# Turning the rows of an FFN by VectorE and DRAM instead of by TensorE

## Chip, cores and metric

The kernel runs on one core of a Trainium2 chip. The metric is the device time of one execution in microseconds (us); "before" is the median of three runs.

## What is computed

Four sequences of 512 rows with 1024 features each go through causal self-attention with 16 heads, a residual and a normalization, then through one dense layer with int8 weights and a scale per output, a residual and a normalization again. In the reference, cut to what matters here:

```python
x = L0_attn_hidden_states                      # (4, 512, 1024) float32
x = _layernorm(x + _L0_attn_ref(x, w_q, w_k, w_v, w_out), axis=-1)
x = _layernorm(x + _L0_ffn_ref(x, weight, scales), axis=-1)

def _L0_ffn_ref(x, weight, scales):
    w_dequant = weight.astype(jnp.float32) * scales.astype(jnp.float32)[:, None]
    return jnp.einsum('bsi,oi->bso', x, w_dequant)
```

The dense layer is called FFN below. Its matmul needs the rows turned: the features, over which it sums, must lie on the 128 partitions.

## The kernel before, in words

All matmuls run in a one-pass float type (`FR`) on numbers that are split into digits, a high part and a low part, so that together they are as exact as float32. What is multiplied is therefore always a set of tiles "h", "l" and, where both sides are split, a difference "d".

**Attention (from the start to about 765 us).** 32 units (a sequence and a pair of heads) go through projection, scores, softmax and the product with the values. The probabilities and the values are turned by VectorE in 32x32 blocks (`turn`, L445 to L450): the blocks are written to a buffer in DRAM and read back by DMAs that put each block in its place (L457 and L467). The outputs of the heads go to DRAM (`ao`). In this stage the order on TensorE, VectorE and ScalarE is written out by hand.

**Output projection and FFN (from about 740 us on).** The 2048 rows are worked in 16 row tiles t of 128 rows. For each t:

- `load_row` (L188) brings the residual rows into one of four buffers, `x_sb[t]`; the four lie in the former tables `cos_sb` and `sin_sb` and in two staging tiles `row`. A buffer is loaded again once the output of the row tile four back is stored (L651, issued by GpSimd).
- `load_ao` (L184) brings the attention output into `raw_ao`; `high_w` (ScalarE, L212 and L213), `low_w` and `diff_w` (VectorE, L217 and L221) split it into `WD[t % 3]`, which holds h, l and d. There are three such sets.
- `out_product` (L190 to L208) multiplies it with the output weight in two halves of 512 columns, 24 matmuls each (L197, tile `y`). VectorE evacuates each half twice (L206) and adds it to the row; after the last evacuation of half 1, `norm` (L106, L112, L114, L115, L108) normalizes the row.
- `transpose_x1` turns the normed row: eight transposes of 128x128 on TensorE into two PSUM tiles `xT` (L624), then for each half a copy to `x1hi` on ScalarE (L626) and the subtraction `x1lo` on VectorE (L627).
- `ffn` multiplies `x1hi` and `x1lo` with the weight `wf` (L638, 2 x 16 matmuls, tile `f`), scales, adds the residual (L646, L647) and normalizes.

The weight `wf` is cast once from int8 words (L599, L605), half of it on VectorE and half on ScalarE.

In this stage only the order on TensorE is written out by hand (`manual_schedule`, L663): the loop at L664 sets it. In iteration t it lists both projection halves of row tile t + 2, the turn of row tile t and the FFN of row tile t. The first and last iterations differ. In t = 0 the halves (1,1), (2,1) and (3,0) are listed (row tile, half), in t = 1 only (3,1). The halves (0,0), (0,1), (1,0) and (2,0) run earlier, between the attention's last units. In t = 13 the last halves (15,0) and (15,1) are listed, so t = 14 and t = 15 consist of the FFN alone. The order on VectorE, ScalarE and the DMA queue of SyncE (SP) is chosen by a scheduler when the kernel is built. Each engine and each queue works through its list in order, so an instruction that waits holds up all that is behind it.

`x1hi` and `x1lo` come from the pool `row` with one buffer each. For row tile 14 the digits go into `WD[1]`, which is free by then; row tile 15 uses `x1hi` and `x1lo` again. The pool `row` takes the memory of the int8 words, so its tiles can be written only after the casts.

Of the kernel before, what the change touches and what calls it, by code (L numbers as in the profile page):

```python
# [9 lines left out]
FP = mybir.dt.float32  # L10
# [5 lines left out]
ALU = mybir.AluOpType  # L16
AX = mybir.AxisListType

P = 128
B, S, E, H, D = 4, 512, 1024, 16, 64  # L20
NC = E // P
# [17 lines left out]
def attention_ffn_kernel(  # L39
# [18 lines left out]
    nc = tc.nc  # L58
    PSUM = bass.MemoryType.PSUM
# [11 lines left out]
    ident = const.tile([P, P], FP, name="ident")  # L71
# [8 lines left out]
    for n in (512, 384):  # L80
# [5 lines left out]
        out=mask,  # L86
        in_=mask,
# [8 lines left out]
    NT_ROWS = B * NI  # L96
    x_sb, row_tiles, oprod = {}, [], {}
# [3 lines left out]
    def norm(r, name, stats=None):  # L101

        if stats is None:
            stats = stp.tile([P, 2, 6], FP, tag="stats", name=f"stats_{name}")
            for n in range(2):
                nc.vector.bn_stats(stats[:, n, :], r[:, ts(n, 512)])  # L106
        mean, rstd = moments(name, stats)
        nc.vector.tensor_scalar(r, r, mean, rstd, ALU.subtract, ALU.mult)  # L108

    def moments(name, stats):  # L110
        mv = stp.tile([P, 2], FP, tag="mv", name=f"mv_{name}")
        nc.vector.bn_aggr(mv, stats)  # L112
        rstd = stp.tile([P, 1], FP, tag="rstd", name=f"rstd_{name}")
        nc.scalar.activation(rstd, mv[:, 1:2], AF.Sqrt, bias=eps_sb)  # L114
        nc.vector.reciprocal(rstd, rstd)  # L115
        return mv[:, 0:1], rstd
# [10 lines left out]
    R, Q = 4, 32  # L127
# [10 lines left out]
    def digits(name, width):  # L138
        pool = ctx.enter_context(tc.tile_pool(name=name, bufs=1, side=RIGHT_SIDE))
        return [pool.tile([P, NC, width], FR, name=f"{name}_{n}") for n in "hld"]  # L140
# [3 lines left out]
    WD = [digits(f"w{k}", P) for k in (2, 1, 0)][::-1]  # L144
# [36 lines left out]
    def load_ao(t, tile=None):  # L181

        tile = staged["w", t % 3] = stage(f"sa_{t}", [P, NC, P]) if tile is None else tile
        nc.sync.dma_start(out=tile, in_=ao[t // NI][:, :, ts(t % NI, P)])  # L184

    def load_row(t):
        x_sb[t] = row_tiles[t % 4]
        nc.sync.dma_start(out=x_sb[t], in_=x[ts(t, P), :])  # L188

    def out_product(t, half, n, pool, tag):  # L190

        w, r = XD[half], WD[t % 3]
        if n in (0, 2 * NC):
            oprod[n > 0] = pool.tile([P, 512], FP, tag=tag, name=f"y_{t}_{half}_{n}")
        ps = oprod[n >= 2 * NC]
        c, part = (n // 2, n % 2) if n < 2 * NC else (n - 2 * NC, 2)
        nc.tensor.matmul(  # L197
            ps,
            lhsT=r[part][:, c, :],
            rhs=w[part][:, c, :],  # L200
            start=n in (0, 2 * NC),
            stop=n in (2 * NC - 1, NT - 1),
        )
        if n in (2 * NC - 1, NT - 1):
            o = x_sb[t][:, ts(half, 512)]
            nc.vector.scalar_tensor_tensor(o, ps, 1.0 + X12 if n < NT - 1 else -X12, o, op0=MUL, op1=ADD)  # L206
            if half and n == NT - 1:
                norm(x_sb[t], f"a{t}")  # L208

    def high_w(k):  # L210
        t = staged["w", k]
        nc.scalar.activation(WD[k][0], t, AF.Copy, scale=LESS)  # L212
        nc.scalar.activation(t, t, AF.Copy, scale=1.0 / X12)  # L213
# [9 lines left out]
    def split_w(k):  # L223
        low_w(k)
        diff_w(k)
# [380 lines left out]
        nc.gpsimd.tensor_copy(sc32, sc_sb)  # L606

    with tc.tile_pool(name="row", bufs=1) as rowp, tc.tile_pool(name="sum", bufs=2) as sump, tc.tile_pool(
        name="ps_x", bufs=2, space=PSUM
    ) as ps_x, tc.tile_pool(name="ps_f", bufs=2, space=PSUM) as ps_f, tc.tile_pool(  # L610
        name="ps_o", bufs=2, space=PSUM
    ) as ps_o:
        x1T = {}

        def transpose_x1(t, digits=None):


            if digits is None:
                digits = [rowp.tile([P, NC, P], FR, tag=f"x1{n}", name=f"x1{n}_{t}") for n in ("hi", "lo")]
            hi, lo = x1T[t] = digits[:2]  # L620
            for n in range(2):
                ps = ps_x.tile([P, 4, P], FP, tag="xT", name=f"xT_{t}_{n}")
                for c in range(4):
                    nc.tensor.transpose(ps[:, c, :], x_sb[t][:, ts(4 * n + c, P)], ident)  # L624
                cs = slice(4 * n, 4 * n + 4)
                nc.scalar.copy(hi[:, cs, :], ps)  # L626
                nc.vector.tensor_tensor(lo[:, cs, :], ps, hi[:, cs, :], ALU.subtract)  # L627

        def ffn(t, last=False):
            hi, lo = x1T.pop(t)  # L630
            r = x_sb.pop(t)
            stats = stp.tile([P, 2, 6], FP, tag="stats", name=f"stats_f{t}")
            for n in range(2):
                o = ts(n, 512)
                ps = ps_f.tile([P, 512], FP, tag="f", name=f"f_{t}_{n}")
                for c in range(NC):
                    for part in (hi, lo):
                        nc.tensor.matmul(  # L638
                            ps,
                            lhsT=part[:, c, :],  # L640
                            rhs=wfv[:, c, o],
                            start=(c == 0 and part is hi),
                            stop=(c == NC - 1 and part is lo),
                        )
                f = sump.tile([P, 512], FP, tag="sum", name=f"fs_{t}_{n}")
                nc.vector.tensor_mul(f, ps, sc32[:, o])  # L646
                nc.vector.tensor_add(r[:, o], f, r[:, o])  # L647
                nc.vector.bn_stats(stats[:, n, :], r[:, o])
            if not last:
                norm(r, f"f{t}", stats)  # L650
                nc.gpsimd.dma_start(out=out[ts(t, P), :], in_=r)  # L651
                return
            mean, rstd = moments(f"f{t}", stats)
            for n, queue in enumerate((nc.sync, nc.scalar)):
                o = ts(n, 512)
                nc.vector.tensor_scalar(r[:, o], r[:, o], mean, rstd, ALU.subtract, ALU.mult)
                queue.dma_start(out=out[ts(t, P), o], in_=r[:, o])

        def out_half(t, half):
            for n in range(NT):  # L660
                out_product(t, half, n, *((pjp, "pj") if half else (ps_o, "o")))

        with tc.manual_schedule(engines={mybir.EngineType.PE}):  # L663
            for t in range(NT_ROWS):  # L664
                early = t + 2
                if 1 < t < NT_ROWS - 2:
                    out_half(early, 0)
                if t + 3 < NT_ROWS:
                    if t:
                        load_row(t + 3)  # L670
                    load_ao(t + 3, raw_ao)
                    high_w(t % 3)
                    split_w(t % 3)
                if t == 0:
                    out_half(1, 1)
                    transpose_x1(0)
                    out_half(2, 1)
                    out_half(3, 0)
                elif early < NT_ROWS:
                    transpose_x1(t)  # L680
                    out_half(early, 1)
                if t == NT_ROWS - 3:

                    transpose_x1(t + 1, WD[t % 3])
                if t == NT_ROWS - 2:
                    transpose_x1(t + 1)
                ffn(t, t == NT_ROWS - 1)


# [44 lines left out]
```

## Time and profile before

| What | Value |
|---|---|
| median of three runs | 1058.34 us (1056.18 to 1058.88) |
| the profiled execution's own time | 1059.0 us |
| its span, first to last instruction | 1057.2 us |
| TensorE (PE) busy | 1013.2 us, 96% |
| VectorE (DVE) busy | 891.1 us, 84% |
| ScalarE (ACT) busy | 384.2 us, 36% |
| GpSimd (POOL) busy | 185.4 us, 18% |
| mean granted TensorE clock | 0.992 |
| share of the chain of waits: the transposes xT, L624 | 1% |
| xT: matmuls, mean length | 128 (in three groups), 272 to 273 ns |
| x1hi copies on ScalarE (L626) | 32, 588 ns |
| x1lo subtractions on VectorE (L627) | 32, 677 ns |

"Busy" is the time in which an engine works on an instruction; matmuls are pipelined, so their lengths overlap and their sum is more than the time they take up. The chain of waits is followed back from the last instruction: at each step it goes to what released it, or to the instruction before it on the same engine. It says which work sets the end. The granted clock is TensorE's clock as a share of full speed.

### The profile page before, as it was taken

To read this page: it belongs to the slowest core of one execution; us is meant where nothing else is said; L and a number is where in the kernel's file an instruction comes from. 1 tells how busy PE (TensorE), PEld (TensorE's weight loads), DVE (VectorE), ACT (ScalarE), POOL (GpSimd) and SP (SyncE) were. 2 spreads that over 40 slices of the span, in tenths; PEclk is the share of its full clock that TensorE was granted. 3 is DMA by queue.
4 is the path that set the end of the run, shared out by engine and by line. 5 is a ranking of instruction groups with operands and counts; after the bars stand their busy time and mean duration, and the time that the engine had idled before them with its cause. 6 is when DMAs were issued, how large, how long until landed. Compare 5 with 4: busy or idle time off the path is not lost.

```text
span 1057.2 us, 13527 instructions
## 1 busy us (share of the span) xinstructions
PE 1013.2 (96%) x4708; PEld 754.4 (71%) x4708; DVE 891.1 (84%) x1386; ACT 384.2 (36%) x854; POOL 185.4 (18%) x281
## 2 busy tenths in 40 slices
PE   9989999999999989999999999988799999999997
PEld 3666777767777667677776777765588888888885
DVE  6998898998989989898898988988897767667666
ACT  5524354343544334444344443443342121121110
POOL 0122232222322222232223322221200000000000
PEclk9999999999999999999999999999999999999999
DMA  6556655766557766566655666577532222221201
GB/s 258 162 186 191 189 179 179 225 194 179 179 181 223 240 203 191 158 209 190 211 187 159 210 195 210 183 214 245 178 120 104 77 100 80 80 80 60 77 23 60
DMA packets 192212, 173.65 MB, mean 164 GB/s; under 512 B 90640, under 2 KB 156688, under 8 KB 192016
## 3 DMA queue, kind: packets, MB, share of 16 engines
q1 hardware_dynamic: 184656, 155.22, 47.0%
q10 hardware_dynamic: 5328, 9.70, 2.5%
q0 software_dynamic: 2160, 7.87, 1.8%
q8 instruction: 37, 0.61, 0.2%
q14 instruction: 31, 0.25, 0.1%
HBM read 105.64 MB, written 67.11 MB: 163 GB/s over the span
## 4 chain that ended last, share of the span: by engine, by line
PE 67%; DVE 21%; ACT 4%; DMA 3%; issue 2%; POOL 0%; SPq 0%; DVEq 0%; ACTq 0%
PE p L267 31%; PE y L197 15%; PE f L638 11%; PE o L475 6%; DVE nmx L415 4%; DVE s L412 3%; DVE w_l L217 3%; DVE w_d L221 2%; PE s L398 2%; DVE pr L448 2%; PE xT L624 1%; ACT sw L213 1%; DVE x_d L175 1%; ACT w_h L212 1%; DVE rot L235 1%
## 5 line engine op out<-in xcount | busy, mean ns | idle before, releaser
L267 PE MATMUL p<-x_h,w_h 128*128 128x512 f32 x736 | 290.5, 395 | 0.0
L267 PE MATMUL p<-x_l,w_l 128*128 128x512 f32 x736 | 287.0, 390 | 0.5 <-DVE w_l L217 0.5
L443 POOL TENSOR_SCALAR pr<-pr,rden 128x128 f32<-128x128 f32 (+3 forms) x256 | 175.0, 703 | 572.1 <-DVE rden L437 533.4
L267 PE MATMUL p<-x_d,w_d 128*128 128x512 f32 x736 | 186.1, 395 | 0.9 <-DVE v L309 0.9
L429 ACT ACTIVATE pr<-s,nmx 128x128 f32<-128x128 f32 (+3 forms) x256 | 132.4, 539 | 147.8 <-DVE nmx L415 111.9
L267 PEld LDWEIGHTS p<-x_h,w_h 128*128 128x128 f32 x736 | 138.1, 188 | 52.5 <-issue 22.7
L267 PEld LDWEIGHTS p<-x_d,w_d 128*128 128x128 f32 x736 | 135.7, 188 | 33.9 <-issue 5.1
L267 PEld LDWEIGHTS p<-x_l,w_l 128*128 128x128 f32 x736 | 138.3, 188 | 28.9 <-DVE w_l L217 0.9
L286 ACT ACTIVATE tA<-p 128x512 f32<-128x512 f32 x92 | 55.8, 606 | 219.2 <-PE p L267 219.2
L197 PE MATMUL y<-x_h,w_h 128*128 128x512 f32 x256 | 102.7, 401 | 4.4 <-DVE row L206 3.9
L415 DVE TENSOR_REDUCE nmx<-s 128x2 f32<-128x256 f32 (+3 forms) x128 | 102.5, 821 | 3.4
L475 PE MATMUL o<-prT,va 128*64 128x256 f32 (+3 forms) x512 | 79.4, 454 | 24.6 <-ACT pr L429 21.2
L197 PE MATMUL y<-x_l,w_l 128*128 128x512 f32 x256 | 101.2, 395 | 1.0 <-DVE w_l L217 1.0
L448 DVE STREAM_TRANSPOSE pr<-pr 128x768 f32<-128x768 f32 (+1 forms) x96 | 100.0, 1049 | 0.9 <-POOL pr L443 0.8
L638 PE MATMUL f<-wf,x1hi 128*128 128x512 f32 x240 | 93.6, 390 | 0.0
L638 PE MATMUL f<-wf,x1lo 128*128 128x512 f32 x240 | 93.6, 390 | 0.0
L475 PEld LDWEIGHTS o<-prT,va 128*64 128x64 f32 x512 | 34.9, 140 | 73.8 <-issue 37.1
L309 DVE SCALAR_TENSOR_TENSOR raw<-p,tA 128x512 f32<-128x512 f32 x61 | 40.2, 659 | 50.8 <-PE p L267 50.8
L398 PE MATMUL s<-qk 64*128 64x384 f32 (+3 forms) x512 | 79.4, 450 | 1.8 <-DVE qk L242 1.8
L221 DVE TENSOR_TENSOR w_d<-w_h,w_l 128x1024 fp32r<-128x1024 f32 x60 | 73.7, 1228 | 1.5
L197 PE MATMUL y<-x_d,w_d 128*128 128x512 f32 x256 | 64.2, 392 | 1.4 <-DVE v L309 0.7
L197 PEld LDWEIGHTS y<-x_h,w_h 128*128 128x128 f32 x256 | 48.7, 190 | 16.0 <-DVE row L206 4.3
(105 smaller groups left out, 1225.2 us busy)
## 6 DMA issues: line engine op xcount, KB each, us to landing
turned<-pr SPq DMA_DIRECT2D x64, 384.0 KB, 2.3
turned<-pr SPq DMA_DIRECT2D x32, 512.0 KB, 3.7
prT<-turned SPq DMA_DIRECT2D x32, 512.0 KB, 4.9
prT<-turned SPq DMA_DIRECT2D x32, 384.0 KB, 4.7
turned_v<-v SPq DMA_DIRECT2D x32, 256.0 KB, 3.3
va<-turned_v SPq DMA_DIRECT2D x128, 64.0 KB, 2.6
prT<-turned SPq DMA_DIRECT2D x32, 256.0 KB, 3.6
ao<-ot ACTq DMA_DIRECT2D x32, 256.0 KB, 2.0
```

The costliest lines, as they stand in the source:

```text
L197: nc.tensor.matmul(ps, lhsT=r[part][:, c, :], rhs=w[part][:, c, :], start=n in (0, 2 * NC), stop=n in (2 * NC - 1, NT - 1),)
L221: nc.vector.tensor_tensor(d, h, l, SUB)
L267: nc.tensor.matmul(ps, lhsT=w[part][:, c, :], rhs=r[part][:, c, :], start=n in (0, 2 * NC), stop=n in (2 * NC - 1, NT - 1),)
L286: nc.scalar.activation(prod["tA"], ps, AF.Copy, scale=1.0 + X12)
L309: nc.vector.scalar_tensor_tensor(raw_tile(u, k), ps, -X12, prod["tA"], op0=MUL, op1=ADD)
L398: nc.tensor.matmul(ps[:, j, at : at + n], lhsT=t[rows, 0, ts(i, P)], rhs=keys[rows, :, : (i + 1) * Q], start=True, stop=True,)
L415: nc.vector.tensor_reduce(nmx[:, 2 * i : 2 * i + 2], ps[:, :, at : at + n], AX.X, ALU.max, negate=True)
L429: nc.scalar.activation(pr[:, :, at // P : at // P + i + 1, j, :], ps[:, j, at : at + n].rearrange("p (r k s) -> p r k s", r=R, s=Q), AF.Ex ...
L443: nc.gpsimd.tensor_scalar(p, p, rden[:, m : m + 1], 1.0, ALU.mult, ALU.mult)
L448: nc.vector.transpose(t, t)
L475: nc.tensor.matmul(ps[j * D : (j + 1) * D, kb * P :], lhsT=v[:, kb, 2 * j : 2 * j + 2, :].rearrange("p a s -> p (a s)"), rhs=t[:, :, 4 * k ...
L638: nc.tensor.matmul(ps, lhsT=part[:, c, :], rhs=wfv[:, c, o], start=(c == 0 and part is hi), stop=(c == NC - 1 and part is lo),)
```

## The change

The normed rows are turned in the way of `turn` in the attention. VectorE turns the row in 32x32 blocks into a new tile `blocks` (one buffer); one DMA of SP writes it to one of two buffers in DRAM, `turned_x`, and four DMAs read it back, each 128 KB in pieces of 32 numbers, straight into `x1lo`. ScalarE then copies the whole tile to `x1hi`, and VectorE subtracts it in place. TensorE takes no part. The two PSUM tiles of the transposes are gone.

Read back in this way the features lie on the partitions in another order: partition p holds the feature p % 4 * 32 + p // 4 of each block of 128. The rows of the int8 weight are put into the same order when the inputs are prepared. The digits of row tile 15 go into `WD[2]` instead of `x1hi` and `x1lo`, and its turn is listed one iteration earlier, beside that of row tile 14.

```diff
         def transpose_x1(t, digits=None):
             if digits is None:
                 digits = [rowp.tile([P, NC, P], FR, tag=f"x1{n}", name=f"x1{n}_{t}") for n in ("hi", "lo")]
             hi, lo = x1T[t] = digits[:2]
-            for n in range(2):
-                ps = ps_x.tile([P, 4, P], FP, tag="xT", name=f"xT_{t}_{n}")
-                for c in range(4):
-                    nc.tensor.transpose(ps[:, c, :], x_sb[t][:, ts(4 * n + c, P)], ident)
-                cs = slice(4 * n, 4 * n + 4)
-                nc.scalar.copy(hi[:, cs, :], ps)
-                nc.vector.tensor_tensor(lo[:, cs, :], ps, hi[:, cs, :], ALU.subtract)
+            blocks = rowp.tile([P, R, NC, Q], FP, tag="blocks", name=f"blocks_{t}")
+            nc.vector.transpose(blocks, x_sb[t].rearrange("p (c r s) -> p r c s", r=R, s=Q))
+            nc.sync.dma_start(
+                out=turned_x[t % 2].rearrange("a (n r) w -> (a n) (r w)", r=R),
+                in_=blocks.rearrange("p r c s -> p (r c s)"),
+            )
+            x1 = lo.bitcast(FP)
+            for a in range(R):
+                nc.sync.dma_start(
+                    out=x1[:, :, ts(a, Q)], in_=turned_x[t % 2][a].rearrange("p (c s) -> p c s", s=Q)
+                )
+            nc.scalar.copy(hi, x1)
+            nc.vector.tensor_tensor(lo, x1, hi, ALU.subtract)
...
                 if t == NT_ROWS - 3:
                     transpose_x1(t + 1, WD[t % 3])
-                if t == NT_ROWS - 2:
-                    transpose_x1(t + 1)
+                    transpose_x1(t + 2, WD[(t + 1) % 3])
                 ffn(t, t == NT_ROWS - 1)
...
-        "w8": rows(L0_ffn_weight).reshape(P, NC * E).view(np.int32),
+        "w8": np.ascontiguousarray(rows(L0_ffn_weight)[np.arange(P) % 4 * 32 + np.arange(P) // 4]).reshape(P, NC * E).view(np.int32),
```

`R` is 4, `Q` is 32, `NC` is 8, `P` is 128 and `NT_ROWS` is 16.

## The prediction, made before the changed kernel ran

> **What bounds the kernel now.** I read the busy table and the chain of waits first, then the chain and the timelines of the stage that the diff touches, from 755 us to the end. The chain of that stage, in order of time (start us, length us, what):
>
> ```profile
> 770.99 0.87 PE xT L624 x8
> 771.87 10.93 PE y L197 x48
> 782.80 7.38 PE f L638 x32
> 790.18 0.87 PE xT L624 x8
> 791.05 5.49 PE y L197 x24
> 796.54 7.26 PE f L638 x32
> 803.80 5.49 PE y L197 x24
> 809.29 0.87 PE xT L624 x8
> ```
>
> TensorE alone carries the chain until 1049.7 us, without a wait between its pieces. One row of steady state is a projection half y (24 matmuls, 5.49), the turn xT (0.87), the other half (5.49) and the FFN f (7.26). VectorE has room, as the busy time by stretch shows (stretch, then PE, PEld, DVE, ACT, POOL busy):
>
> ```profile
> 850.00:870.00 20.00, 20.00 (x93) 16.58 (x92) 13.62 (x23) 3.79 (x6) 0.53 (x1) 1.00 0.27 91
> ```
>
> So a turn taken off TensorE is worth its full chain time, as long as its replacement is ready when TensorE reaches f.
>
> **What is removed.** 128 transposes (16 rows of 8), 32 ScalarE copies (0.59 each) and 32 VectorE subtractions (0.68). Their matmul row by kind reads
>
> ```profile
> L624 PE MATMUL xT<-ident,row 128*128 128x128 f32 x64 | 8.3, 273 | 0.0
> ```
>
> 273 ns each. The Trainium skill ("TensorE: Matmul & The Clock Gate", Part 4: PE-mode transpose) gives a transpose about 275 ns within a kernel. By that length the change would save 128 x 0.273 = 34.9 us. The chain decides otherwise: eight of them take 0.87, since they overlap, so the saving is 16 x 0.87 = **13.9 us**. I take 13.9.
>
> **What is added, per row.** On VectorE one 32x32 turn of 128x1024 (L448 does the same size in 1.24) and one subtraction of 128x1024 (L171: 1.21). On ScalarE one copy of 128x1024 (L212: 1.06). On SP one write of 512 KB to DRAM (row loads of that size land 3.2 after issue, row stores 2.9; I take 3.0; ends 2.3, the 384 KB row of L449, and 3.7, its 512 KB row) and four reads of 128 KB in pieces of 128 bytes. The nearest row to the reads is L467, with pieces of the same size, half as many:
>
> ```profile
> va<-turned_v SPq DMA_DIRECT2D x128, 64.0 KB, 2.6
> raw_ao<-ao SPq DMA_DIRECT2D x13, 512.0 KB, 4.1
> 738.41 2.55 SPq L467 DMA_DIRECT2D va<-turned_v x4
> ```
>
> The last line is SP's timeline (start, length of four issues: 0.64 each). So four va reads are through at 3 x 0.64 + 2.6 = 4.5 us; the DMA share over that time adds up to about 2.0 us of work on all 16 engines. The new reads have twice the pieces, about 4.0 us of work, behind about 1.7 us of latency: **5.7 us** for a set (ends 4.5, as if the pieces cost nothing, and 8, as if issue and work added up). VectorE sees in all 16 x (1.24 + 1.21) - 32 x 0.68 = +17.4 us over some 290 us, which fits into its free third. ScalarE's load hardly moves (16 x 1.06 for 32 x 0.59).
>
> **Where the wait falls.** x1lo and x1hi have one buffer, and the reads land in x1lo. So the reads of row t wait until the FFN of row t-1 has read its last x1lo. From there to the FFN of row t there lie two projection halves, 10.98 us, in rows 2 to 13, but only one, 5.49, in row 1. Before the change the matmul into PSUM needed no such release.
>
> *Rows 2 to 13.* Reads 5.7, copy 1.06, subtraction 1.21, with 0.3 of handovers: 8.3 of 10.98. VectorE's list has the subtraction after the evacuations of projection half 0 (L206, done at about 7.2 by its queue) and ahead of those of half 1 (the first is available at about 9.1), so it is neither late nor in the way. On SP, ahead of the reads stand a row load (it waits for a store that ended some 9 us after the FFN before) and an ao load (issued about 4 us before); both are out of the way. The write of the turned blocks is issued a whole row early. Cost 0, with 2.7 us to spare.
>
> *Row 0.* Here nothing has to be released, but the order does the harm. The timeline of VectorE before:
>
> ```profile
> 776.72 3.34 DVE L605 CAST wf<-words 128x1024 fp32r<-128x1024 int8 x4
> 779.99 0.68 DVE L206 SCALAR_TENSOR_TENSOR row<-y,row 128x512 f32<-128x512 f32 x1
> 780.70 0.69 DVE L106 BATCH_NORM_STATS2 stats_a<-row 128x6 f32<-128x512 f32 x1
> ```
>
> In the changed program's instruction list the turn of row 0 stands behind these three, although row 0 was normed at 769.3: it begins at 781.4 and ends at 782.65. The write lands at 785.75. SP then has the ao load of row 6 ahead of the four reads; it waits for low_w of row 5, which VectorE's list places after the turn and two evacuations: 785.35. So the reads are issued from about 785.95, behind 512 KB whose work is about 2.6 us: 785.4 + 1.7 + 2.6 + 4.0 = 793.7 if they queue wholly, 791.65 if not; I take 793.0. Copy and subtraction: 795.4. TensorE, rid of one turn, is at f at 782.63 - 0.87 = 781.76. **Stall 13.6 us** (ends: write 2.3 and reads 4.1 give 10.7; write 3.7 and full queueing give 15.6).
>
> *Row 1.* From the end of FFN 0: reads 5.8. VectorE takes the rest of FFN 0's norm, two evacuations (L206), low_w and only then the subtraction of row 1. In the trace before, the evacuation of FFN 0's second half starts at 790.21 and low_w ends at 798.4; in that measure, projection half (3,1) ends at 796.4, and the subtraction would end at 799.7. **Stall 3.4** (3.3 to 5).
>
> *Row 15.* The last projection half leaves two FFNs, 14.5 us. Row 14's subtraction is now queued ahead of the last evacuation and holds it about 1.2 us; evacuation and norm 2.9 (1025.94 to 1028.8 without the subtractions); turn 1.24, write 3.0, reads 5.7, copy and subtraction 2.3: 16.4. **Stall 1.9** (0 to 4).
>
> **The clock.** A stall costs more than itself. In TensorE's timeline (start, length, instruction, idle before):
>
> ```profile
> 377.70 4.07 PE L475 MATMUL o<-prT,va 128*64 128x512 f32 x16 [3.43 <-DMA va<-turned_v]
> 755.68 0.50 PE L197 MATMUL y<-x_h,w_h 128*128 128x512 f32 x1 [3.88 <-DVE row L206]
> 756.72 0.57 PE L197 MATMUL y<-x_h,w_h 128*128 128x512 f32 x1
> 760.08 0.44 PE L197 MATMUL y<-x_h,w_h 128*128 128x512 f32 x1
> ```
>
> From 756.72 to 760.08 eight matmuls started 0.42 apart instead of 0.227, at a granted clock of 0.50: 1.6 us lost after 3.88 idle. After 3.43 idle (377.7) the clock was 0.50 again. The skill's rule against the change is in "TensorE: Matmul & The Clock Gate", Why this matters for your kernels: no idle gaps of more than about 3 us. By the rule both stalls, 13.6 and 3.4, are charged: +3.2. By the rows alone the second lies just below the shortest gap of its kind, and the charge could be 1.6. The nearest row is 3.43, so I charge both. Gaps of 1.67 and 2.11 left the clock alone, one of 1.83 (at 56.5) didn't; for row 15 I charge nothing (end 1.6).
>
> **Sum.** -13.9 + 13.6 + 3.4 + 1.9 + 3.2 = **+8.2 us**. On the profiled execution (1059.0, of which the span is 1057.2) that is 1067.2; it lay 0.7 above the median of the runs, so for the median 1058.34 + 8.2 = 1066.5. Low ends: -13.9 + 10.7 + 3.3 + 0 + 1.6 = +1.7, 1060.0. High ends: -13.9 + 15.6 + 5 + 4 + 6.4 (two slow windows after row 0, one after each other stall) = +17, 1075.4.
>
> **Rivals.** A difference below 0.3% (3.2 us) can't be told from none.
>
> 1. *Slower by the stalls of rows 0, 1 and 15*, +8.2: chance 0.70.
> 2. *The cover nearly holds: no change or better.* One mechanism: the round trip of row 0 through DRAM. If the ao load ahead doesn't delay the reads and a set takes 4.5, the first stall is about 11, and with no clock charge for row 1 and row 15 on time the sum is about +2, near 1060.5; it decides from 17 us of stalls and clock charges in all downward, and the change is faster by over 3.2 only from 10.7 downward, which the stall of row 0 alone uses up. For it: the DMA engines are idle three quarters of this stage. Against it: the turn of row 0 waits behind the casts whatever the DMAs do. Chance 0.17, of which 0.06 for faster (about 1050).
> 3. *Every row stalls.* If a set of reads takes over 8.4 us, each of rows 2 to 13 waits, and VectorE's queue is held by the subtraction: at 9.5 about 12 x 1.1 = 13 us more, and two to three more in rows 0 and 15: 1082. For it: pieces of 128 bytes, and SP's issues are in one queue with the ao and row loads. Against it: the va reads. Chance 0.13.
>
> The range takes case 1 with its ends and most of case 2: 1060 to 1075. Slower 0.81, same 0.13, faster 0.06.
>
> **What would show it.** In the profile after: a TensorE gap of 10 to 16 us ahead of the first f, ended by the subtraction into x1lo, then a granted clock of 0.5; a second gap of 3 to 5 ahead of the second f; none in rows 2 to 13, with rows 18.2 apart instead of 19.1; one of about 2 before the last f. A first gap below 6 us, or gaps in the rows between, would prove me wrong, and so would rows that are still 19.1 apart.

## The result, and the profile after

| What | Before | After |
|---|---|---|
| median of four runs | 1058.26 us (1056.18 to 1058.88) | 1067.24 us (1065.45 to 1069.31) |
| ratio of the times | | 1.0086, 95% interval 1.0061 to 1.0111 |
| span of the profiled execution | 1057.2 us | 1067.5 us |
| TensorE busy | 1013.2 us | 1005.4 us |
| VectorE busy | 891.1 us | 908.9 us |
| mean granted TensorE clock | 0.992 | 0.980 |

The change makes the kernel 9.0 us slower by the medians and 10.3 us slower by the two profiled spans. TensorE has less to do and yet ends later, so it waits. The chain of waits of the changed kernel, in the stage that the diff touches (start us, length us, what), shows where:

```profile
777.98 3.33 DVE wf L605 x4
...
782.55 0.15 DVE blocks L624
...
786.48 0.53 SPq L184
...
787.10 0.62 SPq L631
...
790.47 3.64 DMA x1lo<-turned_x
794.21 1.05 ACT x1hi L634
795.29 1.24 DVE x1lo L635
796.57 8.49 PE f L646 x31
...
811.19 1.22 DVE w_l L217
812.40 1.14 DVE x1lo L635
813.59 10.14 PE f L646 x31
823.73 10.92 PE y L197 x48
...
841.92 10.92 PE y L197 x48
```

Before, this stretch was TensorE alone. Now the chain leaves TensorE twice, ahead of the FFN of row 0 and ahead of the FFN of row 1. From row 2 on it is TensorE alone again, and there the rows are 841.92 - 823.73 = 18.19 us apart where they were 19.11. That is 0.92 gained per row, 14.7 in sixteen rows. The two FFNs behind the gaps are also longer: 31 matmuls of 32 (the first one ran within the gap) would take 31/32 of 7.26, which is 7.03, and took 8.49 and 10.14. Not all of that is a slow clock: in five of the kernels below 31 matmuls behind a wait took 7.29 to 7.34 although the granted clock stayed at 1.00.

TensorE's timeline has the same waits with what ended each (start, length, instruction, and in brackets the idle time before it and its releaser):

```profile
795.31 0.79 PE L646 MATMUL f<-wf,x1hi 128*128 128x512 f32 x1 [12.12 <-ACT x1hi L634]
796.57 0.79 PE L646 MATMUL f<-wf,x1lo 128*128 128x512 f32 x1 [0.47 <-DVE x1lo L635]
811.75 0.49 PE L646 MATMUL f<-wf,x1hi 128*128 128x512 f32 x1 [1.21 <-ACT x1hi L634]
813.59 0.79 PE L646 MATMUL f<-wf,x1lo 128*128 128x512 f32 x1 [1.35 <-DVE x1lo L635]
...
1042.66 0.47 PE L646 MATMUL f<-wf,w_h 128*128 128x512 f32 x1 [0.69 <-DVE fs L654]
1051.23 0.49 PE L646 MATMUL f<-wf,w_h 128*128 128x512 f32 x1 [0.86 <-ACT w_h L634]
1052.49 0.50 PE L646 MATMUL f<-wf,w_l 128*128 128x512 f32 x1 [0.77 <-DVE w_l L635]
```

I measure a gap from the end of the work before it to the second matmul of f, the one with x1lo, and take off 0.23 for the first matmul, which runs within it.

- Row 0: from 795.31 - 12.12 = 783.19 to 796.57 is 13.4, net 13.15.
- Row 1: from 810.54 to 813.59 is 3.05, net 2.8.
- Row 15: from 1050.37 to 1052.49 is 2.1, net 1.9.
- Row 14: 0.69 ahead of its f, ended by VectorE's late evacuation of the FFN before it.

Rows 2 to 13 have no wait at all. The granted clock is in the busy time by stretch of the changed kernel (stretch, then length, PE, PEld, DVE, ACT and POOL busy, granted clock, DMA share, GB/s):

```profile
795.30:799.10 3.80, 3.33 (x7) 2.33 (x8) 2.37 (x2) 0.00 (x0) 0.00 (x0) 0.50 0.17 66
813.00:819.40 6.40, 5.81 (x14) 4.55 (x15) 4.60 (x7) 0.29 (x1) 0.00 (x0) 0.50 0.62 199
...
850.00:870.00 20.00, 20.00 (x90) 16.52 (x89) 15.61 (x24) 4.74 (x6) 0.53 (x1) 1.00 0.53 145
```

These stretches lie inside longer spells: the clock is at half from 785.49 to 799.14, of which only the last 2.6 us lie behind the second matmul of row 0's f, and from 812.80 to 819.62, of which 6.0 us do so in row 1. In row 15's FFN it is 1.00 throughout. The last line answers to the one shown of before: in a steady 20 us VectorE is busy 15.6 us instead of 13.6, still with room.

The sum by this trace: -14.7 for the turns, +13.15 + 2.8 + 1.9 + 0.7 for the gaps, +1.5 and +3.1 for the longer FFN 0 and FFN 1 (over 7.03; of this about 1.2 and 2.8 are the slow clock, counted from 7.3), +0.5 for FFN 15 (7.51 for 31 matmuls, at full clock). That is +8.95. The stage began 1.3 us later than its share: the projection half (3,0) ended at 783.19 instead of 782.80, although the turn of row 0, 0.87, was no longer ahead of it. Part of that lies in a stretch from 756 to 764, where 24 matmuls of y took 8.32 instead of 7.34 behind the same gap of 3.88: the clock is at half for 6.8 us there (754.77 to 761.60), before for 3.4 (756.77 to 760.18). Together +10.2, against 10.3 between the spans.

### The profile page after: what moved, and what is told of

It is laid out like the page before. It is cut to its first block, busy times and chain, and to the rows that moved or that the text cites. A ratio compares the mean times of both kernels' runs of the same rounds, so it can differ in the third digit from the quotient of the medians.

```text
span 1067.5 us, 13475 instructions
## 1 busy us (share of the span) xinstructions
PE 1005.4 (94%) x4580; PEld 744.6 (70%) x4580; DVE 908.9 (85%) x1386; ACT 384.0 (36%) x838; POOL 186.1 (17%) x281
## 4 chain that ended last, share of the span: by engine, by line
PE 62%; DVE 23%; DMA 6%; ACT 5%; issue 3%; SPq 1%; POOL 0%; DVEq 0%; ACTq 0%
PE p L267 31%; PE y L197 13%; PE f L646 10%; PE o L475 6%; DVE nmx L415 4%; DVE w_l L217 3%; DVE s L412 3%; PE s L398 2%; DVE w_d L221 2%; DVE pr L448 2%; DVE x_l L171 1%; ACT sw L213 1%; ACT w_h L212 1%; DVE x_d L175 1%; DVE rot L235 1%
## 5 line engine op out<-in xcount | busy, mean ns | idle before, releaser
L646 PE MATMUL f<-wf,x1hi 128*128 128x512 f32 x224 | 89.9, 401 | 13.3 <-ACT x1hi L634 13.3
L646 PE MATMUL f<-wf,x1lo 128*128 128x512 f32 x224 | 89.9, 401 | 1.8 <-DVE x1lo L635 1.8
```

The lines of the kernel that those rows point to most:

```text
L646: nc.tensor.matmul(ps, lhsT=part[:, c, :], rhs=wfv[:, c, o], start=(c == 0 and part is hi), stop=(c == NC - 1 and part is lo),)
```

## The experiments

My theory after this profile: the gain is the chain time of the transposes, about 0.9 per row, and it is given back at the edges of the stage, in rows 0, 1 and 15 and in the clock after their gaps, while rows 2 to 13 hide the round trip with about 2.5 us to spare. The rivals: the gain is something else than the chain time; every row loses a little; or a single link (the place of the turn in VectorE's list, the ao load ahead of the reads on SP, the one buffer of x1lo) carries the loss alone.

### No turn at all

The kernel before, with the transposes left out: the FFN multiplies the rows unturned, so the output is not the reference's. No replacement is put in.

```diff
-                ps = ps_x.tile([P, 4, P], FP, tag="xT", name=f"xT_{t}_{n}")
-                for c in range(4):
-                    nc.tensor.transpose(ps[:, c, :], x_sb[t][:, ts(4 * n + c, P)], ident)
+                ps = x_sb[t][:, ts(n, 512)].rearrange("p (c s) -> p c s", s=P)
```

> The kernel before, with the 128 transposes left out: x1hi and x1lo are made from the rows as they lie, so the FFN multiplies unturned rows. It measures the gain by itself. Theory: the transposes are worth their chain time, 16 x 0.92 us as read from the distance of the rows (19.11 before, 18.19 after), so 1058.3 - 14.7 = 1043.6 us, rows 18.2 apart, no TensorE wait in the FFN stage. Rival: they are worth their mean length, 128 x 0.273 = 34.9 us, so 1023 us. Rival: something else sets the pace once they are gone (VectorE), so above 1050 us.

Measured: 1042.61 us (1042.23 to 1045.14), ratio 0.9856 (0.9829 to 0.9883), 15 to 16 us below before. The rows are 18.18 apart, as in the changed kernel. So the most that the turn could give back is 15 to 16 us, close to the chain time of 14.7, and not the 34.9 us that the lengths of the transposes add up to.

### The reads twice

The changed kernel, with every set of four reads made twice into the same tile.

```diff
-            for a in range(R):
+            for a in [*range(R), *range(R)]:
```

> The changed kernel with each of the four reads of a row issued twice into the same place. Theory: rows 2 to 13 are hidden with some 2.5 us to spare; a set of reads grows from 5.4 to about 9.5 us, the chain to 12.1 us against 10.92 us of cover, so about 1.2 us of TensorE gap now stands in every row, 14 us in rows 2 to 13, about 4 us more in each of rows 0, 1 and 15, and clock charges on top: 1090 us or more. Rival (the reads are far from any limit, only the order at the ends counts): no gap in rows 2 to 13, about 1079 us.

Measured: 1104.44 us (1101.75 to 1106.52), ratio 1.0434 (1.0402 to 1.0465). Now rows 2 to 13 do wait. TensorE's timeline of this kernel, one such row:

```profile
860.77 0.50 PE L646 MATMUL f<-wf,x1hi 128*128 128x512 f32 x1 [0.39 <-ACT x1hi L634]
862.03 0.50 PE L646 MATMUL f<-wf,x1lo 128*128 128x512 f32 x1 [0.76 <-DVE x1lo L635]
```

The row before has its second matmul of f at 842.13, so these two are 19.90 apart, 1.7 more than in the changed kernel, where I had expected 1.2 (over ten rows, to 1042.89, 20.1 on average). The doubled reads are issued over 7.47 us from 849.49 instead of 2.9, and row 0's gap grows from 13.4 to 16.4 (781.65 to 798.10), row 1's from 3.05 to 7.0. A set takes 5.4 us in the changed kernel (823.76 to about 829.1) and here 10.2 (849.49 to 859.7, where the copy to x1hi begins). Of the 4.8 added, 1.7 show as a wait; some 3 were free. That is the slack of these rows; the edge rows have none.

### Rows 0 and 1 left to TensorE

The changed kernel, but rows 0 and 1 are turned by TensorE as before. The features must then lie in the natural order, so the write to DRAM puts them there with four DMAs and the rows of the weight aren't reordered.

```diff
+            if t in (0, 1):
+                for n in range(2):
+                    ps = ps_x.tile([P, 4, P], FP, tag="xT", name=f"xT_{t}_{n}")
...
+                return
...
-            nc.sync.dma_start(
-                out=turned_x[t % 2].rearrange("a (n r) w -> (a n) (r w)", r=R),
-                in_=blocks.rearrange("p r c s -> p (r c s)"),
-            )
+            for a in range(R):
+                nc.sync.dma_start(
+                    out=turned_x[t % 2][a].rearrange("(r n) w -> n r w", r=R),
+                    in_=blocks[ts(a, Q)].rearrange("p r c s -> p r (c s)"),
+                )
...
-        "w8": np.ascontiguousarray(rows(L0_ffn_weight)[np.arange(P) % 4 * 32 + np.arange(P) // 4]).reshape(P, NC * E).view(np.int32),
+        "w8": rows(L0_ffn_weight).reshape(P, NC * E).view(np.int32),
```

> Rows 0 and 1 turned by TensorE as before, rows 2 to 15 by VectorE and DRAM; for that the blocks are written to DRAM in natural order by four DMAs, and the weight keeps its order. Theory (the loss sits in rows 0 and 1, 13.4 and 3.0 us of gap and 1.5 and 3.1 us of slow clock): 1058.3 - 14 x 0.92 + 2.5 for row 15 = 1048 us. Rival (the way through DRAM slows every row or the whole stage): 1058 us or more.

Measured: 1050.60 us (1049.34 to 1053.55), ratio 0.9922 (0.9892 to 0.9952). Without the two edge rows the change gains. It missed the expected 1048 by the last row: TensorE's timeline has no gap in rows 0 and 1, and one of 3.4 ahead of the last f, whose 31 matmuls then took 9.06, 2.0 over 7.03. By terms: 14 x -0.92 + 3.4 + 2.0 = -7.5; the medians give -8.0 (1058.62 before, beside these runs).

### Two buffers for x1lo

```diff
-                digits = [rowp.tile([P, NC, P], FR, tag=f"x1{n}", name=f"x1{n}_{t}") for n in ("hi", "lo")]
+                digits = [
+                    rowp.tile([P, NC, P], FR, tag=f"x1{n}", name=f"x1{n}_{t}", bufs=k) for n, k in (("hi", 1), ("lo", 2))
+                ]
```

The pool `sum` gave up one of its two buffers to make room.

> The changed kernel with two buffers for x1lo (room is made by one buffer instead of two for the scaled FFN output, which only VectorE touches). Theory (row 1 waits because its reads may start only when FFN 0 has ended): the gap before the second FFN and the slow clock after it go, 3.0 + 3.1 us, row 0 stays at 13.4 us of gap, row 15 comes about 1 us earlier: 1060 to 1061 us. Rival (row 1 waits for the order of ScalarE's and VectorE's lists, not for the release): 1066 to 1067 us.

Measured: 1059.14 us (1055.39 to 1061.46, twelve runs), ratio 1.0006 (0.9992 to 1.0020). Row 0's gap stays, 12.8 (781.37 to 794.17), followed by an FFN of 8.68. Rows 1 and 15 wait no longer, as the chain shows:

```profile
808.33 7.26 PE f L648 x32
...
1026.57 22.44 PE f L648 x96
```

Row 1's reads are issued at 793.16, before FFN 0 begins, and no longer at its end (805.09 in the changed kernel). Row 15 has no digits in x1lo and still gains its whole wait, where I had expected about 1 us. The SP timeline of the changed kernel shows how:

```profile
1023.82 3.01 SPq L631 DMA_DIRECT2D x1lo<-turned_x  x4
1026.88 4.20 SPq L631 DMA_DIRECT2D w_l<-turned_x  x4
```

The first line is row 13's set of reads, which waited for FFN 12 to end; row 14's set stands behind it in the list and lands at 1035.3. VectorE, whose list has row 14's subtraction ahead, therefore evacuates the last projection half only at 1037.63, 2.9 us after it was ready (1034.7), and row 15's turn comes late. With two buffers row 14's reads are issued at 1015.38, right behind their write. So the gaps of rows 1 and 15 with their longer FFNs, 2.8 + 3.1 + 1.9 + 0.5 = 8.3 us in the changed kernel, go with the second buffer. The sum, -14.7 + 12.8 - 0.23 + 1.65 for FFN 0 and 0.66 for the last three (22.44 against 21.78), is +0.2.

### Row 0 turned early

The turn of row 0 is issued ahead of the load of the int8 words, and `x1lo` and `blocks` get memory that isn't shared with the words.

```diff
+    transpose_x1(0)
+    with tc.tile_pool(name="words", bufs=1) as wordsp:
...
-                    transpose_x1(0)
+                    split_x1(0)
```

> The changed kernel with the turn of row 0 emitted before the load of the int8 words, and with x1lo and blocks in memory of their own, so that they needn't wait for the casts; nothing else moves. Theory (row 0 is late because its turn stands behind the casts in VectorE's list and its reads behind an ao load on SP): the turn starts at about 773 instead of 782.5, the write and reads queue behind the words (1 MB), the subtraction ends some 8 to 10 us earlier, so the gap before the first FFN shrinks from 13.4 to 4 or 5 us; 1058 us. Rival (the round trip through DRAM is itself too long to hide at this place): a gap of 10 us or more, 1065 us.

Measured: 1058.26 us (1055.17 to 1062.23, twelve runs), ratio 0.9998 (0.9983 to 1.0014). The turn starts at 773.97 instead of 782.55, and row 0's gap falls from 13.4 to 4.5 (784.21 to 788.73):

```profile
773.97 1.23 DVE L611 STREAM_TRANSPOSE blocks<-cos_sb 128x1024 f32<-128x1024 f32 x1
```

The early start is thus worth 8.9 us. This run moves two things at once: the turn's place in VectorE's list, and the memory of `blocks` and `x1lo`, which in the changed kernel lies under the int8 words, so that the turn can't start before the casts end (781.4) whatever the list says. Behind the casts the list holds it for another 1.2 us at most. The reads also go ahead of the ao load of row 6 here. The rest of the changed kernel's loss remains: FFN 0 takes 9.49, row 1's gap is 3.05 with an FFN of 8.95, row 15's 1.5. In the new gap the write takes 4.72 from its issue and the reads 6.3 (779.97 to 786.27), beside the words, the scales and an ao load on the same engines.

### The ao load of row 6 on another queue

The changed kernel; only this one load is issued by GpSimd instead of SP, so that it is no longer ahead of the reads in their queue.

```diff
-        nc.sync.dma_start(out=tile, in_=ao[t // NI][:, :, ts(t % NI, P)])
+        (nc.gpsimd if t == 6 else nc.sync).dma_start(out=tile, in_=ao[t // NI][:, :, ts(t % NI, P)])
```

> The changed kernel with the ao load of row 6 issued by GpSimd instead of SP, so that it no longer stands ahead of row 0's reads in SP's list. Theory (most of the 13.4 us gap is the late turn and the round trip; the load ahead is worth what it holds SP and the DMA engines, 1 to 2 us): a gap of 11.5 to 12.5 us. Rival (the load ahead is the main cause): a gap below 8 us.

Measured in one run: 1064.09 us. Both expectations failed for row 0: its gap is 13.4 as before (782.19 to 795.64). Its chain of waits:

```profile
782.87 2.61 DMA turned_x<-blocks
...
785.49 0.53 SPq L631
...
787.49 5.70 DMA x1lo<-turned_x
```

The reads are indeed issued at once when the write has landed, 785.49, in 2.86 us. But they land only at 793.2, 7.7 us after the start of the first, where a set in steady state takes 5.4. GpSimd issued the ao load at 786.08, 0.6 after the first read, and SP the next row's block write at 788.40. From 787 to 793 the DMA engines' share was 1.09 at 223 GB/s, against 0.53 in a steady 20 us. Out of the queue, the same 512 KB are still in flight beside the reads. The run is 3.2 below the changed kernel's median. What shows for it is not in row 0: row 1's gap, 3.1 (809.56 to 812.62), was followed by an FFN of 7.32 instead of 10.14.

### The features in natural order, nothing else

The changed kernel with the four DMAs of the write and the weight in its own order, as in the kernel with rows 0 and 1 on TensorE, but all rows turned by VectorE.

> The changed kernel with the blocks written to DRAM in natural order by four DMAs of 1 KB pieces instead of one of 4 KB pieces, and the weight in its own order; everything else as changed. It is the part that the runs with rows on TensorE share. Theory (the write isn't on the path in rows 2 to 13): rows 18.2 apart and no gap there; gaps of rows 0, 1 and 15 as in the changed kernel within 2 us, except where the new list of VectorE moves the last subtraction: 1066 to 1070 us. Rival (the four writes delay each row): gaps in rows 2 to 13, 1075 us or more.

Measured in one run: 1065.98 us. Rows 2 to 13 are 18.18 apart without a gap, so four writes cost no more than one there. In row 0 the gap is 10.65 (780.28 to 790.93), 2.7 shorter, which is outside the 2 us that I had allowed. SP's timeline of this kernel (start, length, instruction) shows why:

```profile
782.86 2.87 SPq L632 DMA_DIRECT2D x1lo<-turned_x  x4
...
788.54 0.52 SPq L184 DMA_DIRECT2D raw_ao<-ao  x1
```

Here the scheduler put the ao load behind the reads. It is issued at 788.54, when they have landed (788.4, 5.5 after the first). Of the 2.7, the reads themselves give 1.5 (5.5 instead of 7.0) and their earlier issue 1.3: the first read comes 1.98 after the first write was issued, against 3.30 in the changed kernel (783.80 to 787.10). A part of these 1.3 is due to the four writes, since each read here needs only one of them. With the run before, which has 7.7, the ao load is worth some 1.5 to 2.2 us when its bytes are not in flight beside the reads, nothing when only its queue is another. The size rests on two single runs, each of which changes more than the load. The last row waits 3.2 for its subtraction, and the FFN behind it takes 9.05.

### Row 0 to TensorE, two buffers for x1lo

Natural order, rows turned by TensorE: row 0 alone; the buffers as in the kernel with two of x1lo.

> Row 0 turned by TensorE as before, rows 1 to 15 by VectorE and DRAM with two buffers for x1lo (blocks written in natural order by four DMAs). Theory (nothing but rows 0, 1 and 15 cost): no TensorE gap in the FFN stage, the time of the kernel without transposes plus one turn, 1042.6 + 0.9 = 1043.5 us, up to 1046 us if the four writes per row delay a row. Rival (the way through DRAM costs every row something): above 1050 us.

Measured: 1051.52 us (1049.18 to 1053.47), ratio 0.9927 (0.9902 to 0.9952), 5.5 to 8 us above what was expected and, by the number alone, on the rival's side. The trace speaks against the rival: no row from 1 to 14 has a gap. Row 0's gap is 1.5, ended by its subtraction, which stands behind the casts in VectorE's list; the last f waits 3.1 and then takes 10.15, 3.1 over 7.03. ScalarE had copied the row at 1029.06. VectorE's timeline of this kernel (start, length, instruction) shows what the subtraction waited for:

```profile
1030.67 0.69 DVE L667 TENSOR_TENSOR fs<-f,sc 128x512 f32<-128x512 f32 x1 [1.58 <-PE f L659]
...
1032.73 1.21 DVE L648 TENSOR_TENSOR w_l<-w_l,w_h 128x1024 fp32r<-128x1024 f32 x1
```

VectorE stood idle for 1.58 until FFN 14's second half was done, with the ready subtraction (the last line) behind it in its list. A list, not a transfer, held the last row. The kernel with natural order and nothing else has the same wait, and with one write and two buffers it is absent, so it comes with the four writes; that they moved the scheduler's order is my reading of these three lists.

### Rows 0 and 15 to TensorE, two buffers for x1lo

The kernel above, with row 15 left to TensorE as well, at the place it had before; its digits go into `WD[2]`.

```diff
-            if t in (0,):
+            if t in (0, 15):
...
-                    transpose_x1(t + 2, WD[(t + 1) % 3])
+                if t == NT_ROWS - 2:
+                    transpose_x1(t + 1, WD[(t + 0) % 3])
```

> As the kernel with row 0 on TensorE and two buffers for x1lo, but row 15 is also turned by TensorE, at the place where the kernel before had it. Theory (what was left there is the gap of 3.4 us before the last FFN, made by VectorE's list, which has the last subtraction behind the work on FFN 14, and 3.1 us of slow clock after it): 1051.5 - 6.5 + 0.9 = 1046 us, no gap after row 0. Rival (the end isn't worth that; the way through DRAM costs elsewhere): 1050 us or more.

Measured: 1046.06 us (1044.94 to 1046.73), ratio to before 0.9882 (0.9861 to 0.9902). It beats both kernels. Its chain of waits at the two ends of the stage:

```profile
783.29 7.30 PE f L659 x31
...
1021.59 0.87 PE xT L630 x8
1022.46 14.94 PE f L659 x64
```

No row waits but row 0, for 1.74 ahead of the first line, and the clock stays whole: FFN 0 takes 7.30 for 31 matmuls. By terms 14 x -0.92 + 1.7 = -11.2; the medians differ by 12.3 (1058.40 before, beside these runs), and the last 1.1 is not traced.

## Why the prediction was right

The time, 1066.5 against 1067.24, and the place of each loss came as said. That the times lie so close is in part luck, since errors of 1 to 2 us in the terms cancel. Step by step:

- *The gain is 16 x 0.87, by the chain and not by the lengths.* Confirmed: 0.92 per row. The term was 0.05 too small; the first matmul behind a turn is slower as well (it was 0.32 ahead of the next one, not 0.227), so a part of the cost stood in the projection halves (5.49 each, 10.92 for two without a turn). The kernel without any turn shows the same distance of rows.
- *Rows 2 to 13 hide the round trip with 2.7 us to spare.* Confirmed by the rows without a gap, and by the doubled reads, which show some 3 us of slack. A set of reads took 5.4 (predicted 5.7; no run shows its two parts, 1.7 of latency and 4.0 of work, by themselves).
- *Row 0 stalls for 13.6.* Measured 13.15, and the largest link is the one named, the late turn behind the casts: an early turn takes away 8.9. I put it down to VectorE's list alone; the memory shared with the words holds the turn as well, and no run separates the two. The turn began at 782.55 instead of 781.4, and TensorE reached the gap at 783.2 instead of 781.8: both carry the late start of the stage, so the two shifts nearly cancel.
- *In row 0, the ao load ahead on SP delays the reads.* As a matter of order in the queue this fell: on another queue it changed nothing. The reads took 7.0 from their first issue (787.10 to 794.1), 7.7 with the load on another queue, and 5.5 where the load came after them. So it is the 512 KB in flight beside them that delays them; the price I gave it, about 1.35 of a possible 2.05, was somewhat low against 1.5 to 2.2.
- *Row 1 stalls for 3.4, by the single buffer and VectorE's list.* Measured 2.8. Two buffers take it away, so the buffer is shown. The chain has low_w (L217) directly ahead of the subtraction, as said.
- *Row 15 stalls for 1.9.* Measured 1.9, and another 0.7 ahead of row 14's f, which I had not seen: VectorE evacuated the FFN before it late. The mechanism was the one named, row 14's subtraction ahead of the last evacuation, but it held that for 2.9 us and not 1.2, because row 14's reads stood behind row 13's on SP. That the row's own stall still came to 1.9 is luck: a part of the longer delay showed ahead of row 14 instead.
- *The clock costs 2 x 1.6.* The mis-sized term. FFN 0 was 1.5 longer than 7.03, FFN 1 3.1 and FFN 15, charged at nothing, 0.5: 5.1 for 3.2. The slow clock is about 1.2 and 2.8 of that. The other 1.1, by which an FFN behind a gap is longer at full clock too (0.3 twice, 0.5 in row 15), had no term in the prediction. Row 0 paid for less than one spell of 3.4 us, since most of its slow time fell into the gap itself; row 1 paid for nearly two. The rule that I weighed there (no gaps of more than about 3 us) doesn't decide such a gap, nor does its length: behind gaps of 3.05, 3.05, 3.05 and 3.1 in four kernels FFN 1 took 10.14, 8.95, 8.91 and 7.32. What decides is under the last heading.

The errors went both ways. The rows gained 0.8 more than said, rows 0 and 1 waited 1.05 less, row 14 and the longer FFNs cost 0.7 and 1.9 more: +8.95 for +8.2 in the stage. The remaining 1.3 of the span came ahead of the stage, about 1.0 of it in the slow spell around 760. I have no experiment on it; the profiled execution was also the slowest of the four, 2.1 above the median.

The rival without stalls lost because row 0's round trip can't begin early enough: even begun 8.6 us earlier, it leaves 4.5. The rival in which every row stalls lost on the length of a set of reads, whose turning point is about 5.4 + 3 = 8.4, as put.

## What to carry to other kernels

Price a step that is taken off the bounding engine by its time in the chain, not by the lengths of its instructions, and then look for the replacement at the ends of the loop: a round trip that steady state hides is bare in the first row, in the row with half the distance, and in the last. Leave such rows on the old path or give them a second buffer, and keep the new path for the rest; here rows 0 and 15 on TensorE and two buffers for row 1 turned a loss of 9 us into a gain of 12. Look also at where each replacement stands in the other engines' lists, since a ready 1.2 us subtraction behind one waiting evacuation cost 3.1 us of wait and nearly as much again (2.8) in clock.

## What the hardware showed that I had not expected

- Gaps of the same length on TensorE cost very different amounts of clock. The Trainium skill ("TensorE: Matmul & The Clock Gate", Part 1: The HAM clock gate) says that the clock is set by activity in a free-running window of about 3.4 us. The traces agree: while TensorE has work, every slow spell lasts a whole multiple of 3.41 us, and within one run their starts are whole multiples of 3.41 us apart (in the changed kernel 754.77, 785.49, 812.80). Row 1 of four kernels, with the matmuls' busy time in the window that holds most of the gap:

| Kernel | Row 1's gap | That window: busy of 3.41 us | Clock after it | FFN 1, 31 matmuls |
|---|---|---|---|---|
| turn early | 803.70 to 806.75 | 803.60 to 807.01: 0.86 | 0.50 for 3.4 us | 8.95 |
| natural order | 806.21 to 809.26 | 806.48 to 809.89: 1.12 | 0.50 for 3.4 us | 8.91 |
| changed | 810.54 to 813.59 | 809.39 to 812.80: 1.65 | 0.50 for 6.8 us | 10.14 |
| ao load moved | 809.56 to 812.62 | 808.28 to 811.69: 1.79 | 1.00 | 7.32 |

- So a gap is paid for when it takes up more than about half of one window. In the clock records of the eleven traces of this case, all 59 windows at full clock with less than 1.45 us of matmuls were followed by half clock, and none with more than 1.66 was; between these both happened. In the changed kernel the gap reached 0.8 us into the next window, which had 2.6 us of matmuls at half clock, and the clock stayed at half for one more; in the two kernels above it that window was full of matmuls and the clock came back. That is read from the traces; no run here moved a gap within its window on purpose. It means that a change can shift by some 3 us through nothing but the place of a gap.
- Two gaps of 0.39 and 0.76 in each row of the kernel with doubled reads cost no clock at all: 7.34 for 31 matmuls.
- DMAs on different queues took as much from each other as on one. Reads of 4 x 128 KB in pieces of 128 bytes took 5.4 to 5.5 us with only the next row's write behind them, and 7.0 to 7.7 with a 512 KB load in flight as well, whichever queue issued it.
